# A third tile for block results, a later third sum, and two layer norms from statistics of halves, in a two-layer graph kernel

## The chip, the cores and the metric

The kernel runs on one core of one Trainium2 chip. A core has TensorE (PE: matrix products into PSUM; its weight loads are shown as PEld), VectorE (DVE), ScalarE (ACT), GpSimd (POOL, which here does nothing in layers 0 and 1 but issue gathers and scatters) and SyncE (SP, which issues the plain transfers). The metric is the device time of one execution in microseconds, the median of several runs; smaller is better.

## The reference

x has 2708 rows of 1024 float32, adj is a sparse 0/1 matrix of 2708 by 2708. Two layers follow each other, each with a residual and a layer norm:

```
# layer 0: attention over the neighbours in adj
q = x @ W_q.T + b_q;  k = x @ W_k.T + b_k;  v = x @ W_v.T + b_v
z = (q @ k.T) / sqrt(1024) * adj;   z = where(z == 0, -10000, z)
x1 = layernorm(x + relu(softmax(z) @ v))
# layer 1: sum over the neighbours
out = layernorm(x1 + adj @ (x1 @ weight) + bias)
```

The norm is (x - mean) / sqrt(var + 1e-5) over a row's 1024 elements, without weights.

## The kernel before

The work is cut into 22 blocks of 128 rows (the last, block 21, has 20). Because adj is sparse, each row's neighbours are listed, the rows are sorted by their number, and a block needs as many row gathers ("slots") as its fullest row has neighbours: `SLOTS` gives 15, 11, 8, ... for the blocks, 13 for block 8, 1 for blocks 18 to 20, 0 for block 21.

**Before 530 us** the kernel lists the neighbours, forms M = W_q.T W_k, and computes y = x M block by block (`y_block`), which is stored to DRAM in two parts, `y_ds`, for the first 8 blocks and the others. With y, a row's scores are dot products with the gathered rows of x.

**Layer 0, attention.** For a block, `attend` gathers y's rows (`gather_y`) and, slot by slot, rows of x (g tiles, 9 buffers, line 349), takes the scores on VectorE (line 792), turns them to probabilities, and sums the gathered rows with them into r (line 849). `flip` transposes r on TensorE (line 716), and r is multiplied by W_v. Blocks 0 to 6 and 21 do so alone (`project`, then `finish0`, lines 879 to 891); the other fourteen in seven pairs (`pairs`, first (7, 20), then (19, 18), last (13, 12)). For a pair the 2x2 block product over two blocks of rows and halves of the contraction and of the columns is done with seven half products instead of eight (`pair_products`, line 991 on; its matmuls are on line 976), which need four differences of the operands (`turn_pair`: S[0] to S[3] in s_all, lines 965 to 968) and four of the weights (lines 1107 to 1110). Each half product's PSUM bank is read out by an addition on VectorE at line 988 into a tile t. `finish_pair` adds the row of x with relu (line 1045), calls `norm` (lines 767 to 789) and scatters the block to x1 in DRAM (`scatter`, line 703). In `norm` ScalarE squares the whole row to get the variance (line 775), takes a logarithm and an exponential for the root (778, 780), VectorE mends these by one step (782 to 787), and ScalarE applies the norm to 1024 columns (788).

The tile t of the single blocks and of a pair's first block comes from the pool wp with two buffers; a pair's second comes from the pool xb with two. xb is opened where y's buffers (pool xa) lay, once y is done. A tile's next user waits until the scatter of the last one has landed.

**Layer 1, plain sums.** It works in units: (20,), (19, 18), (17, 16), (15, 1), ..., the last (12, 13). `sum_rows` gathers a block's neighbours of x1 and adds them up in r (lines 1209 and 1211), `gather_x1` fetches the block's own rows with the bias already in the tile (line 1218, then a gather that accumulates), `turn1` transposes and forms the differences, `work1` makes the products and adds the residual (line 1242), and `finish1` norms and scatters to the output. In the loop over units, unit i's products run after the next unit's transposes and after the sums for a unit further ahead have been put into the queues; the third unit's sums (got1[2]) are put ahead of the loop.

**What sets the order.** Each engine works through its queue in order. A scheduler lays the queues out from the program's order, from priorities (`tc.high_priority(URGENT)`, around evictions of PSUM) and from hints made with `follow`, which puts one instruction behind another on the same engine. So an instruction that waits holds up all that stand behind it on its engine.

Of the kernel before, what the change touches and what calls it, by code (L numbers as in the profile page):

```python
# [9 lines left out]
F32 = mybir.dt.float32  # L10
# [4 lines left out]
AF = mybir.ActivationFunctionType  # L15
ALU = mybir.AluOpType
# [4 lines left out]
P = 128  # L21
EPS = 1e-5
MASKED = -10000.0
FAR = 1.0e30
HALF = 512
# [55 lines left out]
def sparse_part(ctx, tc, x, xT, adj, wqT, wkT, wvT, bq, bk, bv, w1, b1, out):  # L81
    nc = tc.nc
    N, D = x.shape
    DC = D // P
    NH = D // HALF
    scale = 1.0 / math.sqrt(D)
# [11 lines left out]
    last = [b for b in range(NB) if SLOTS[b] == 0]  # L98
# [12 lines left out]
    with es:  # L111
        const = es.enter_context(tc.tile_pool(name="const", bufs=1))
        stat = es.enter_context(tc.tile_pool(name="stat", bufs=4))
# [34 lines left out]
        eps = const.tile([P, 1], F32, name="eps")  # L148
# [54 lines left out]
        loaded, sorted_, products, applied = [], [], [], []  # L203
# [54 lines left out]
        for c in range(DC):  # L258
            nc.vector.scalar_tensor_tensor(junk[:, :D], wq_i[c // 2][:, c % 2, :], scale, bk_bc, op0=ALU.mult,
                                           op1=ALU.mult, accum_out=u_col[:, c:c + 1])  # L260
# [75 lines left out]
        def follow(later, earlier, same=False):  # L336

            kind = mybir.DependencyClass.NoSync if same else mybir.DependencyClass.Sync
            tc.add_manual_dep(later.ins, earlier.ins.name, mybir.DependencyInfo(kind, mybir.DependencyReason.DATA),
                              reason="an engine's queue shall not stand still for a transfer")  # L340
# [346 lines left out]
        put = row_constants(0)  # L687
# [79 lines left out]
        def norm(t, sm, n, sm2=None):  # L767
# [20 lines left out]
            applied.append(nc.scalar.activation(t[:n], t[:n], AF.Identity, bias=nmr[:n], scale=rstd[:n]))  # L788
            return end

        def score(yg, xg, s, n):
            nc.vector.scalar_tensor_tensor(junkv[:n], yg[:n, :D], scale, xg[:n], op0=ALU.mult, op1=ALU.mult,  # L792
                                           accum_out=s)
# [84 lines left out]

        def finish0(b, po, xr):
            n = rows[b]  # L880
            t = wp.tile([P, D], F32, name="t")
            for h in range(NH):
                hs = slice(h * HALF, (h + 1) * HALF)
                with tc.high_priority(URGENT):
                    nc.vector.tensor_add(t[:n, hs], po[h][:n], bias_bc[:n, hs])
            sm = stat.tile([P, 1], F32, name="sm")
            nc.vector.scalar_tensor_tensor(t[:n], t[:n], 0.0, xr[:n], op0=ALU.max, op1=ALU.add, accum_out=sm[:n])
            end = norm(t, sm, n)
            scatter(x1_d[:, :], b, n, t, "x1")
            return end  # L890
# [60 lines left out]
            yield  # L951


        def turn_pair(flips, pool):

            A = []
            for k, flip_to in enumerate(flips):
                rT = (pool if k else wp).tile([P, DC, P], F32, name="rT", bufs=2)
                A.append(flip_to(rT))
            if len(flips) == 1:  # L960
                return A, None
            (a11, a12), (a21, a22) = [(a[:, :DC // 2], a[:, DC // 2:]) for a in A]
            s_all = wm_pool.tile([P, 4, DC // 2, P], F32, name="s_all", tag="m3")
            S = [s_all[:, i] for i in range(4)]
            nc.vector.tensor_add(S[0], a21, a22)
            nc.vector.tensor_sub(S[1], S[0], a11)
            nc.vector.tensor_sub(S[2], a11, a21)
            nc.vector.tensor_sub(S[3], a12, S[1])
            return A, S

        def differences():
# [8 lines left out]
        def halves_of(t):  # L980
            return t[:, :HALF], t[:, HALF:]
# [46 lines left out]
            return a[:, :DC // 2], a[:, DC // 2:]  # L1028

        def project_pair(pair, A, S):  # L1030
            ts = [(xb_pools[0] if k else wp).tile([P, D], F32, name="t", bufs=2) for k in range(2)]
            bias = halves_of(bias_bc)

            def whole(k, h, acc, what):
                add(halves_of(ts[k])[h], acc, what)

            pair_products(A, S, wv_q, wv_t, [bias, bias], [halves_of(t) for t in ts], whole, pair == pairs[-1])
            return ts

        def finish_pair(pair, ts):  # L1040
            for k, (b, t) in enumerate(zip(pair, ts)):
                xr, sums = pair_x[b], [stat.tile([P, 1], F32, name=f"sm{h}", bufs=6) for h in range(NH)]
                for h in (0, 1) if k == 0 else (1, 0):
                    th = halves_of(t)[h]
                    nc.vector.scalar_tensor_tensor(th, th, 0.0, halves_of(xr)[h], op0=ALU.max, op1=ALU.add, accum_out=sums[h])
                norm(t, sums[0], P, sums[1])
                scatter(x1_d[:, :], b, P, t, "x1")


# [144 lines left out]
        last_norm = applied[-1]  # L1194
        firsts = []

        def sum_rows(b, k=0):
            if b == "hub":
                n, tab, ok, r = P, tab_h, valid_h, part
            else:  # L1200
                n, tab, ok = (P, tab0, valid0) if b == 0 else (rows[b], tabs[:, b, :SLOTS[b]], valid[:, b, :SLOTS[b]])
                r = (cp if k else wp).tile([P, D], F32, name="r", bufs=RB)
            for j in range(tab.shape[1] if b else J0):
                if j == 0 and b not in [0, "hub"] + single + MIXED:
                    gather_slot(x1_d[:, :], tab[:n, 0:1], n, r)
                    continue
                xg = gather_slot(x1_d[:, :], tab[:n, j:j + 1], n, g_tile())
                if j == 0:
                    firsts.append(nc.vector.tensor_scalar(r[:n], xg[:n], ok[:n, 0:1], None, op0=ALU.mult))
                else:  # L1210
                    nc.vector.scalar_tensor_tensor(r[:n], xg[:n], ok[:n, j:j + 1], r[:n], op0=ALU.mult, op1=ALU.add)  # L1211
            return r

        def gather_x1(b, k=0):

            n = rows[b]
            xr = (cp if k else wp).tile([P, D], F32, name="xr", bufs=2 if k else 3)
            follow(nc.scalar.copy(xr[:n], bias1[:n]), last_norm, same=True)
            return gather_at(x1_d[:, :], tabs[:n, b, ROW:ROW + 1], n, xr, ALU.add)

        def finish1(b, t, sums):

            n = rows[b]
            if sums is None:
                sums = [stat.tile([P, 1], F32, name=f"sm{h}", bufs=6) for h in range(NH)]
                for h in range(NH):
                    nc.scalar.activation(junks[:n, :HALF], halves_of(t)[h][:n], AF.Copy, accum_out=sums[h][:n])
            norm(t, sums[0], n, sums[1])
            scatter(out, b, n, t, "out")

        def turn1(unit, rs):
# [3 lines left out]
        def work1(unit, A, S, xrs):  # L1235

            ts = [wp.tile([P, D], F32, name="t", tag="t" if k % 2 == 0 else "yg") for k, _ in enumerate(unit)]
            sums = [[stat.tile([P, 1], F32, name=f"sm{h}", bufs=6) for h in range(NH)] for _ in unit]

            def whole(k, h, acc, what):  # L1240
                with tc.high_priority(URGENT):
                    nc.vector.scalar_tensor_tensor(halves_of(ts[k])[h], acc, 1.0, what, op0=ALU.mult, op1=ALU.add,
                                                   accum_out=sums[k][h])

            xs_ = [halves_of(xr) for xr in xrs]
            if S is None:
                (a11, a12), x0 = halves_of_turned(A[0]), xs_[0]
                pa, pb = bank(), bank()
                half_products(pa, a11, w11, stop=False)
                add(x0[1], pa, x0[1])  # L1250
                half_products(pb, a11, t1, stop=False)
                half_products(pb, a12, w22, start=False)
                whole(0, 1, pb, x0[1])
                half_products(pa, a12, w21, start=False)
                whole(0, 0, pa, x0[0])
            else:
                pair_products(A, S, w1_q, w1_t, xs_, xs_, whole, unit == units[-1])
            return ts, sums
# [7 lines left out]
        nc.vector.tensor_sub(t3, t2, w11)  # L1266
        nc.vector.tensor_sub(t4, w21, t2)
        xrs = {0: [gather_x1(b, k) for k, b in enumerate(units[0])]}
        got1[2] = [sum_rows(b, k) for k, b in enumerate(units[2])]
        for i, unit in enumerate(units):  # L1270
            for p in pending:
                finish1(*p)
            if i + 1 < len(units):
                turned1[i + 1] = turn1(units[i + 1], got1.pop(i + 1))
                xrs[i + 1] = [gather_x1(b, k) for k, b in enumerate(units[i + 1])]
            if i + 3 < len(units):
                got1[i + 3] = [sum_rows(b, k) for k, b in enumerate(units[i + 3])]
            if i == 4:
                sum_rows("hub")
            pending = list(zip(unit, *work1(unit, *turned1.pop(i), xrs.pop(i))))  # L1280
            if i == 2:
                for b in last:
                    pending.append((b, gather_x1(b), None))
# [319 lines left out]
```

## Time and profile before

| | |
|---|---|
| time, median of 3 | 1079.57 us (1079.15 to 1083.0) |
| span of the profiled run | 1076.9 us |
| TensorE busy | 1007.8 us, 94% |
| VectorE busy | 847.2 us, 79% |
| ScalarE busy | 428.4 us, 40% |
| GpSimd busy | 490.7 us, 46% |
| layer 0's last product ends, layer 1's first transpose starts | 757.8, 770.3 us |
| last matmul ends, last scatter issued | 1058.8, 1064.0 us |

TensorE is busy for 94% of the span, so that the time is that of its products and of the few places in which it stands still. Such a place is found in the table of waits, and what ended it in the timeline: the number in brackets is the engine's idle time before the instruction, and after the arrow stands what released it. A share of busy time over the whole span tells little about a stage: VectorE is busy for 79% of it, but for nearly all of some stretches.

### The profile page before, as it was taken

How to read it: one execution, taken by the hardware profiler on the slowest of the kernel's cores; microseconds unless marked ns; L12 is line 12 of the kernel's file. 1: busy time of each engine (PE TensorE's matmuls, PEld its weight loads, DVE VectorE, ACT ScalarE, POOL GpSimd, SP SyncE). 2: the span in 40 equal slices, each digit the busy share in tenths (PEclk: the TensorE clock that was granted, in tenths of full speed). 3: DMA queues.
4: the chain of work that ended last, by engine and by line, in shares of the span. 5: the costliest groups of instructions: out<-in, count | busy, mean ns of one | idle time of the engine just before them, and what ended most of it. 6: DMA issues, size and time to landing. Idle time of an engine off the chain costs nothing.

```text
span 1076.9 us, 10217 instructions
## 1 busy us (share of the span) xinstructions
PE 1007.8 (94%) x2849; PEld 475.1 (44%) x2849; DVE 847.2 (79%) x1825; ACT 428.4 (40%) x898; POOL 490.7 (46%) x397
## 2 busy tenths in 40 slices
PE   7999999999998999999997999899489999999993
PEld 6444444444443444444543444444244444454441
DVE  8799999994388889998497999874578777887431
ACT  4688698422132332224433344332422363333322
POOL 1000140057564536435246566611477777887300
PEclk9999999999999999999998999999899999999997
DMA  9555457564886756796422677735589589969601
GB/s 355 199 206 203 173 196 273 170 244 125 300 279 225 240 191 189 229 334 198 149 92 86 205 255 268 235 118 193 167 284 256 199 269 324 293 204 329 179 39 42
DMA packets 90963, 229.20 MB, mean 213 GB/s; under 512 B 18410, under 2 KB 40394, under 8 KB 88188
## 3 DMA queue, kind: packets, MB, share of 16 engines
q0 software_dynamic: 48768, 148.05, 43.0%
q1 hardware_dynamic: 42128, 80.41, 21.7%
q8 instruction: 24, 0.39, 0.1%
q14 instruction: 43, 0.35, 0.1%
HBM read 219.61 MB, written 33.68 MB: 235 GB/s over the span
## 4 chain that ended last, share of the span: by engine, by line
PE 18%; issue 12%; DVE 11%; DMA 4%; POOL 3%; ACT 2%; POOLq 0%; DVEq 0%; ACTq 0%
PE po L976 16%; DVE junkv L792 2%; DVE r L849 2%; DMA g<-x_d,tabs 2%; DVE r L1211 1%; DMA yg<-y_d,tabs 1%; ACT junks L775 1%; DVE t L988 1%; POOL xr L343 1%; PE tr L716 1%; POOL g L349 1%; POOL x_d L703 1%; PE po L739 1%; PE tr L729 1%; POOL r L349 1%
## 5 line engine op out<-in xcount | busy, mean ns | idle before, releaser
L319 PE MATMUL po<-m_sb,xt 128*128 128x512 f32 x672 | 292.2, 594 | 3.3 <-DVE yo L323 3.3
L319 PEld LDWEIGHTS po<-m_sb,xt 128*128 128x128 f32 x672 | 126.4, 190 | 159.6 <-issue 150.8
L792 DVE SCALAR_TENSOR_TENSOR junkv<-yg,g 128x1024 uint8<-128x1024 f32 x109 | 133.1, 1221 | 36.3 <-DMA yg<-y_d,tabs 16.6
L349 POOL DMA_INDIRECT g<-in_x_dram,tabs x86 | 115.9, 1347 | 76.1 <-DVE r L849 19.4
L976 PE MATMUL po<-t,s_all 128*128 128x512 f32 x272 | 125.5, 604 | 10.9 <-DVE t L988 6.6
L1211 DVE SCALAR_TENSOR_TENSOR r<-g,valid,r 128x1024 f32<-128x1024 f32 x77 | 98.6, 1281 | 18.1 <-DMA g<-x_d,tabs 17.2
L609 PE MATMUL po<-wk_o,wq_o 128*128 128x512 f32 x256 | 110.5, 592 | 0.0
L775 ACT ACTIVATE junks<-t,lnm 128x1024 uint8<-128x1024 f32 (+1 forms) x43 | 49.3, 1146 | 135.2 <-DVE lnm L773 104.7
L739 PE MATMUL po<-wv,rT 128*128 128x512 f32 x224 | 97.7, 594 | 3.3 <-DVE pr L834 2.8
L976 PE MATMUL po<-w,rT 128*128 128x512 f32 x192 | 87.8, 607 | 0.0
L976 PEld LDWEIGHTS po<-t,s_all 128*128 128x128 f32 x272 | 52.0, 194 | 78.4 <-issue 60.7
L563 POOL DMA_INDIRECT tab_d<-rec,pos_i x22 | 27.1, 1230 | 129.9 <-DVE pos_i L552 123.5
L849 DVE SCALAR_TENSOR_TENSOR r<-g,pr,r 128x1024 f32<-128x1024 f32 x64 | 81.9, 1279 | 5.5 <-ACT r L861 4.6
L349 POOL DMA_INDIRECT g<-x_d,tabs x67 | 75.0, 1120 | 22.7 <-issue 15.5
L332 ACT ACTIVATE junka<-xt 128x128 f32<-128x128 f32 x176 | 53.8, 306 | 72.0 <-PE po L319 55.5
L788 ACT ACTIVATE t<-t,nmr,rstd 128x1024 f32<-128x1024 f32 (+1 forms) x43 | 52.6, 1238 | 73.8 <-DVE nmr L787 73.7
L224 DVE MAX8 few<-a 128x8 f32<-128x75 f32 (+3 forms) x132 | 79.2, 618 | 0.0
L609 PEld LDWEIGHTS po<-wk_o,wq_o 128*128 128x128 f32 x256 | 48.4, 190 | 59.3 <-issue 59.0
L976 PE MATMUL po<-w,s_all 128*128 128x512 f32 x160 | 72.1, 592 | 0.0
L221 DVE SCALAR_TENSOR_TENSOR a<-a,iota 128x2708 f32<-128x2708 f32 (+1 forms) x22 | 65.2, 2963 | 5.4 <-ACT junk L220 5.4
L739 PEld LDWEIGHTS po<-wv,rT 128*128 128x128 f32 x224 | 42.3, 190 | 56.3 <-issue 55.2
L219 ACT ACTIVATE junk<-a 128x2708 uint8<-128x2708 f32 (+1 forms) x22 | 54.1, 2459 | 24.7 <-DMA a<-in_adj_dram 20.1
(339 smaller groups left out, 1503.3 us busy)
## 6 DMA issues: line engine op xcount, KB each, us to landing
a<-in_adj_dram SPq DMA_DIRECT2D x21, 1354.0 KB, 5.9
xt<-in_xT_dram SPq DMA_DIRECT2D x21, 512.0 KB, 4.8
y_d<-yo SPq DMA_DIRECT2D x21, 512.0 KB, 5.7
g<-in_x_dram SPq DMA_DIRECT2D x21, 512.0 KB, 7.7
wq_i<-in_wqT_dram SPq DMA_DIRECT2D x8, 512.0 KB, 9.3
wk_i<-in_wkT_dram SPq DMA_DIRECT2D x8, 512.0 KB, 10.4
wv<-in_wvT_dram SPq DMA_DIRECT2D x16, 256.0 KB, 6.0
w<-in_w_dram SPq DMA_DIRECT2D x4, 1024.0 KB, 7.6
```

The lines of the kernel that those rows point to most:

```text
L219: nc.scalar.activation(junk[:n], a[:n], AF.Sign, accum_out=cnt[:n, b:b + 1])
L221: nc.vector.scalar_tensor_tensor(a[:n], a[:n], 1.0, iota[:n], op0=ALU.is_equal, op1=ALU.mult)
L224: nc.vector.max(few[:n, i * 8:(i + 1) * 8], a[:n, cuts[i]:cuts[i + 1]])
L319: put = nc.tensor.matmul(po, xt[:, c, :], m_sb[c // 2][:, c % 2, k0:k1], start=(c == 0), stop=(c == DC - 1))
L349: nc.gpsimd.indirect_dma_start(out=dst[:n], out_offset=None, in_=src, in_offset=bass.IndirectOffsetOnAxis(ap=at, axis=0), bounds_check=N - ...
L609: nc.tensor.matmul(po, wq_o[i // 2][:, o, i % 2 * P:(i % 2 + 1) * P], wk_o[:, o, hs], start=(o == 0), stop=(o == DC - 1))
L739: put = nc.tensor.matmul(acc, rT[:, c, :], w[c // 4][h][:, c % 4, :], start=(c == 0), stop=(c == DC - 1))
L775: nc.scalar.activation(junks[:n], t[:n], AF.Square, bias=nm[:n], accum_out=vs[:n])
L792: nc.vector.scalar_tensor_tensor(junkv[:n], yg[:n, :D], scale, xg[:n], op0=ALU.mult, op1=ALU.mult, accum_out=s)
L849: nc.vector.scalar_tensor_tensor(r[:n], xg[j][:n], pr[:n, j:j + 1], r[:n], op0=ALU.mult, op1=ALU.add)
L976: put = nc.tensor.matmul(acc, a[:, k], w[:, k], start=start and k == 0, stop=stop and k == DC // 2 - 1, skip_group_check=True)
L1211: nc.vector.scalar_tensor_tensor(r[:n], xg[:n], ok[:n, j:j + 1], r[:n], op0=ALU.mult, op1=ALU.add)
```

## The change

It has three parts.

- **A third tile.** The t of blocks 0 and 21 is now taken from xb, where t has three buffers instead of two. The wp pool's two buffers are then free for the first pairs, whose t need not wait for the scatters of blocks 0 and 21.
- **The third unit's sums.** got1[2] moves from ahead of the loop into its first turn, after the second unit's transposes, differences and own rows, and its first addition is put behind the last of the differences (S[3]) on VectorE.
- **The last norms.** For the second block of layer 0's last pair and of layer 1's last unit, the mean and variance come from VectorE's statistics of each half of the row, taken as each half is ready (`bn_stats`), and put together by `bn_aggr`. The norm's application is split: ScalarE does one half of the columns, VectorE the other. The computation of the root is the same.

```diff
+        def norm_halves(t, stats):
+            mv = stat.tile([P, 2], F32, name="mv")
+            nc.vector.bn_aggr(out=mv, in_=stats.rearrange("p h e -> p (h e)"))
+            lv = stat.tile([P, 1], F32, name="lv")
+            nc.scalar.activation(lv, mv[:, 1:2], AF.Ln, bias=eps)
+            near = stat.tile([P, 1], F32, name="near")
+            nc.scalar.activation(near, lv, AF.Exp, scale=-0.5)
...
+            applied.append(nc.scalar.activation(t[:, :HALF], t[:, :HALF], AF.Identity, bias=nmr, scale=rstd))
+            nc.vector.tensor_scalar(t[:, HALF:], t[:, HALF:], rstd, nmr, op0=ALU.mult, op1=ALU.add)
...
         def finish0(b, po, xr):
             n = rows[b]
-            t = wp.tile([P, D], F32, name="t")
+            t = xb_pools[0].tile([P, D], F32, name="t", bufs=3) if b in [0] + last else wp.tile([P, D], F32, name="t")
...
-            nc.vector.tensor_sub(S[3], a12, S[1])
+            halves_turned.append(nc.vector.tensor_sub(S[3], a12, S[1]))
...
-            ts = [(xb_pools[0] if k else wp).tile([P, D], F32, name="t", bufs=2) for k in range(2)]
+            ts = [(xb_pools[0] if k else wp).tile([P, D], F32, name="t", bufs=2 + k) for k in range(2)]
...
         def finish_pair(pair, ts):
             for k, (b, t) in enumerate(zip(pair, ts)):
+                ends = half_stats() if k and pair == pairs[-1] else None
...
+                    if ends is not None:
+                        nc.vector.bn_stats(out=ends[:, h, :], in_=th)
-                norm(t, sums[0], P, sums[1])
+                if ends is None:
+                    norm(t, sums[0], P, sums[1])
+                else:
+                    norm_halves(t, ends)
...
-        def sum_rows(b, k=0):
+        def sum_rows(b, k=0, behind=None):
...
+                if behind is not None:
+                    follow(put, behind, same=True)
+                    behind = None
...
+                    if k and unit == units[-1]:
+                        if len(sums[k]) == NH:
+                            sums[k].append(half_stats())
+                        nc.vector.bn_stats(out=sums[k][-1][:, h, :], in_=halves_of(ts[k])[h])
...
-        got1[2] = [sum_rows(b, k) for k, b in enumerate(units[2])]
         for i, unit in enumerate(units):
             for p in pending:
                 finish1(*p)
             if i + 1 < len(units):
                 turned1[i + 1] = turn1(units[i + 1], got1.pop(i + 1))
                 xrs[i + 1] = [gather_x1(b, k) for k, b in enumerate(units[i + 1])]
+            if i == 0:
+                got1[2] = [sum_rows(b, k, halves_turned[-1]) for k, b in enumerate(units[2])]
```

More of the change, by code (lines that the diff above doesn't have):

```diff
@@ L789, in norm, with half_stats @@
             return end
+        def norm_halves(t, stats):
[5 more added lines that the diff above has]
+            nc.scalar.activation(near, lv, AF.Exp, scale=-0.5)
+            ve = stat.tile([P, 1], F32, name="ve")
+            nc.vector.scalar_tensor_tensor(ve, mv[:, 1:2], EPS, near, op0=ALU.add, op1=ALU.mult)
+            nc.vector.tensor_scalar(ve, ve, near, -0.5, op0=ALU.mult, op1=ALU.mult)
+            rstd = stat.tile([P, 1], F32, name="rstd")
+            nc.vector.scalar_tensor_tensor(rstd, ve, 1.5, near, op0=ALU.add, op1=ALU.mult)
+            nmr = stat.tile([P, 1], F32, name="nmr")
+            nc.vector.scalar_tensor_tensor(nmr, mv[:, 0:1], -1.0, rstd, op0=ALU.mult, op1=ALU.mult)
+            applied.append(nc.scalar.activation(t[:, :HALF], t[:, :HALF], AF.Identity, bias=nmr, scale=rstd))
+            nc.vector.tensor_scalar(t[:, HALF:], t[:, HALF:], rstd, nmr, op0=ALU.mult, op1=ALU.add)
+        def half_stats():
+            return stat.tile([P, NH, nc.vector.BN_STATS_DIM], F32, name="halves", bufs=2)
         def score(yg, xg, s, n):
@@ L951, in attend_shares @@
             yield
+        halves_turned = []
         def turn_pair(flips, pool):
@@ L1208, in sum_rows @@
                 if j == 0:
-                    firsts.append(nc.vector.tensor_scalar(r[:n], xg[:n], ok[:n, 0:1], None, op0=ALU.mult))
-                else:
-                    nc.vector.scalar_tensor_tensor(r[:n], xg[:n], ok[:n, j:j + 1], r[:n], op0=ALU.mult, op1=ALU.add)
+                    put = nc.vector.tensor_scalar(r[:n], xg[:n], ok[:n, 0:1], None, op0=ALU.mult)
+                    firsts.append(put)
+                else:
+                    put = nc.vector.scalar_tensor_tensor(r[:n], xg[:n], ok[:n, j:j + 1], r[:n], op0=ALU.mult, op1=ALU.add)
+                if behind is not None:
+                    follow(put, behind, same=True)
+                    behind = None
             return r
@@ L1227, in finish1 @@
                     nc.scalar.activation(junks[:n, :HALF], halves_of(t)[h][:n], AF.Copy, accum_out=sums[h][:n])
-            norm(t, sums[0], n, sums[1])
+            if len(sums) == NH:
+                norm(t, sums[0], n, sums[1])
+            else:
+                norm_halves(t, sums[-1])
             scatter(out, b, n, t, "out")
```

## The prediction

> **What bounds the kernel now.** First the page's busy times, then TensorE's waits (columns: who waited, for whom, us in total, times, longest), since an edit off TensorE pays only where TensorE stood still.
>
> ```profile
> PE 1007.8 (94%) x2849; PEld 475.1 (44%) x2849; DVE 847.2 (79%) x1825; ACT 428.4 (40%) x898; POOL 490.7 (46%) x397
> ```
>
> ```profile
> PE tr L716 <- DVE r L1209: 13.7, 3, 12.5
> PE po L976 <- DVE t L988: 7.0, 2, 6.6
> PE po L976 <- DVE xr L988: 4.3, 3, 3.0
> ```
>
> TensorE is busy 94% of the span, and its three largest waits are where the change works: 12.5 us at the border of the layers, 6.6 us once in layer 0, 3.0 us once in layer 1. The timeline around the 6.6 us (start, length, engine, line, operation, and in brackets the idle time before it and its releaser):
>
> ```profile
> 569.87 7.48 POOL L349 DMA_INDIRECT g<-in_x_dram,tabs  x1 [0.30 <-DVE rstd L785]
> ...
> 578.89 1.00 POOL L703 DMA_INDIRECT x_d<-t,tabs  x1 [0.30 <-issue]
> ...
> 583.37 1.29 DVE L988 TENSOR_TENSOR t<-po,bias_bc 128x512 f32<-128x512 f32 x2 [6.90 <-DMA x_d<-t,tabs]
> 584.12 6.08 PE L976 MATMUL po<-t,s_all 128*128 128x512 f32 x8 [6.60 <-DVE t L988]
> ```
>
> VectorE reaches the first eviction of the first pair (block 7's t) and waits 6.9 us for the scatter of block 0, which still owns one of the two wp tiles named t. That scatter is issued only at 578.89, behind a gather that held GpSimd for 7.48 us. TensorE waits 6.6 us with it, and its next 8 matmuls take 6.08 us, where 8 take 3.60 elsewhere. The windows (length, busy time and count per engine, granted clock, DMA share, GB/s) tell who limits the stretch after it:
>
> ```profile
> 569.40:603.10 33.70, 27.10 (x64) 12.12 (x63) 25.40 (x52) 8.19 (x15) 19.77 (x12) 0.90 0.42 129
> 600.00:660.00 60.00, 59.68 (x170) 28.29 (x169) 59.61 (x133) 24.70 (x47) 39.33 (x31) 1.00 0.75 246
> ```
>
> From 600 to 660 us VectorE (third figure, 59.61 of 60) is as full as TensorE: what is won at 584 us is kept only as far as VectorE, too, runs earlier. TensorE's waits between 600 and 760 us confirm it: they are on VectorE's probabilities.
>
> ```profile
> PE tr L716 <- DVE pr L834: 2.4, 1, 2.4
> PE tr L716 <- DVE nms L819: 0.8, 1, 0.8
> ```
>
> Layer 1's start and the end:
>
> ```profile
> 786.32 1.29 DVE L1211 SCALAR_TENSOR_TENSOR r<-g,valid,r 128x1024 f32<-128x1024 f32 x1 [1.93 <-DMA g<-x_d,tabs]
> ...
> 789.80 1.99 PE L716 MATMUL tr<-ident,r 128*128 128x128 f32 x16
> ...
> 800.91 0.69 DVE L988 TENSOR_TENSOR xr<-po,xr 128x512 f32<-128x512 f32 x1
> ```
>
> ```profile
> 1058.84 0.69 DVE L1242 SCALAR_TENSOR_TENSOR t<-po,xr 128x512 f32<-128x512 f32 x1 [2.02 <-PE po L976]
> ...
> 1059.82 1.15 ACT L775 ACTIVATE junks<-t,lnm 128x1024 uint8<-128x1024 f32 x1 [2.95 <-DVE lnm L773]
> 1060.87 0.19 ACT L775 ACTIVATION_READ_ACCUMULATOR junks<-t,lnm 128x1 f32 x1
> 1061.09 0.29 ACT L778 ACTIVATE lv<-vs,eps 128x1 f32<-128x1 f32 x1
> ...
> 1062.49 1.24 ACT L788 ACTIVATE t<-t,nmr,rstd 128x1024 f32<-128x1024 f32 x1 [0.87 <-DVE nmr L787]
> 1064.00 0.95 POOL L703 DMA_INDIRECT out_dram<-t,tabs  x1 [5.91 <-ACT t L788]
> ```
>
> From the last eviction (1058.84) to the last scatter (1064.00) 5.16 us pass with nothing beside them; the same chain at the border runs from 757.75 to 763.64, 5.89 us.
>
> [...]6.08 against 3.60 us for 8 matmuls after the 6.6 us wait, 2.5 us of penalty. [...]the 7.48 us gather lay under L1109 and L1110 (two tensor_tensor of 2048, 2.3 us each) and ended 0.95 us after VectorE went idle, but at 609 to 615 us gathers took 1.0 to 1.4 beside two-input SCALAR_TENSOR_TENSORs. [...]
>
> **Part 1, the third tile t.** Blocks 0 and 21 take their t from the xb pool (now 3 buffers). So block 7 takes wp's t after block 2, block 19 after block 1, both scattered long before: the DMA wait is gone, and with it the 6.9 us. The xb tiles lie where layer 0's y buffers lay; in the built program block 21's first eviction now also waits for y's stores, but these had released a y gather at 526.87, and that eviction runs at 563: free. In the built order the pair's first L988 stands straight behind the second operands' last difference (569.4 us), and the pair's products run in their plain order.
> What follows, by durations of the trace: on VectorE from 569.4 to the second pair's first eviction lie 25.4 us of work in 33.7 us, so 8.3 us are idle (6.9 for the scatter, 1.1 for the cold matmuls, rest small). Going through the new order instruction by instruction I find VectorE at that eviction near 596 instead of 603.13, waiting for nothing: 7.1 to 7.5 us earlier. TensorE: the 4 products of 3.43 us from 572.2, with the fifth (a22 with t4) to 589.5, a transpose of 1.0 and two products of the next pair to 597.5, against 606.36: 8.9 us. The smaller counts, since VectorE is full until 660. Against it stands GpSimd: block 8's last gather, in the trace issued at 580.20, must land before VectorE wants it at 589. VectorE no longer goes idle at 576[...]. If a gather takes 2 us instead of 1, it is issued near 583 and lands near 588: just in time. Bounds: loss 0 to 4 us; I take 0.5. **Part 1: 6.8 us, from 3 to 8.9.** After 707 us TensorE runs without waiting to the layer's end, so that the gain is handed on whole.
>
> **Part 2, the third sums behind the second differences.** In the built order GpSimd now issues the second unit's two row gathers (xr, L1218's with accumulation) ahead of the third unit's four gathers, and VectorE makes the second differences before the third unit's two sums (L1211); the L988 that TensorE waits 3.0 us for keeps its place behind the fourth unit's sums, and these keep their place among the gathers. So 801.66 stays. What moves is the wait: the third unit's last gather goes from 779.24 to about 784.8, lands some 5 us after its issue ends, near 791, is summed by 792.4, and the transposes that began at 789.80 wait about 2.6 us; then 1 us of transposes and 7.03 us of products end near 800.8, where they meet the same L988. A wait of 3 us is turned into one of about 2.6 plus 0.9. **Part 2: 0, from a gain of 1 to a loss of 2.**
>
> **Part 3, norms by statistics of halves** (the pair's second block in both layers). Removed from the chain: lnm 0.25, Square 1.05 and its accumulator 0.22, so 1.52 us from 1059.57 to 1061.09. Added: one bn_stats of 512 behind the last eviction (no row of it; lower bound the 0.61 step of a 512 tensor_tensor, upper bound twice that, 1.2; I take 0.65, one pass over one input) and an aggregate, 0.25 like the small steps there: 0.9. The first half's statistics lie in a wait for TensorE (2.02 us before 1058.84), or, at the border, delay the other block's nmr by 0.6, whose scatter then issues near 758.9, before GpSimd is needed for the last. The apply goes from 1.24 on ScalarE to halves on two engines: about 0.65. Saving 0.6 + 0.55 = 1.15 each, 0.5 to 1.3. **Twice: 2.2 us**, both on the chain.
>
> **Sum.** 6.8 + 0 + 2.2 = 9.0 off 1079.57: about **1070.6 us**.
>
> **Rivals.** (a) A gather takes the scatter's place: VectorE at 589 us waits for block 8's last rows[...]; for it speaks the 7.48 us[...]. Part 1 then gives 3, the sum 5.2 or, with part 2 losing 1, 4: 1075.5. (b) VectorE is no limit after 600, since new slack appears at the two waits for yg (2.9 and 1.9 us): all 8.9 are kept, 8.9 + 2.2 + 0.5: 1068. (c) Slower: the denser stretch wins nothing (a new wait of 6.9 us elsewhere in the reordered 600 to 700), part 2 costs its 2 us and more because row gathers with accumulation stand before plain ones and DMA is 91% busy from 770 to 802, and statistics at 1.2 us save nothing: 1079.6 + 5 = 1085. Against it: no new wait of VectorE on a DMA that is late by the trace.
>
> **How the numbers follow.** Forecast 0.60, (a) 0.22, (b) 0.11, (c) 0.07. The bound of faster by over 0.5% is 1074.2: the forecast and (b) lie under it, with some of their spread over it, and a little of (a) under it: 0.74. Within 0.5%: 0.19; slower: 0.07. Range: from (b) less a little, 1066.5, to the middle of (a) and beyond, 1076.5.
>
> **What would show it.** Part 1 right: VectorE's wait for x_d<-t at L988 gone, no clock loss near 585, the second pair's first matmul on t2 near 597 to 598, and layer 0's last matmul near 751. Wrong: a wait of DVE for g or xr between 575 and 605, or TensorE waiting for transposes of block 8's r. Part 2: the 3.0 us wait on L988 becomes one on L716 for the third unit's r. Part 3: last eviction to last scatter 4.0 instead of 5.16. The prediction fails if bn_stats is far over 1.2 us, or if the reordered evictions cost TensorE new waits between 600 and 700.

## The result, and the profile after

The changed kernel takes 1067.62 us (median, 1065.79 to 1069.95) against 1079.86 us of the kernel before: a ratio of 0.9882, 95% interval 0.9855 to 0.991; the medians lie 12.2 us apart. The profiled span goes from 1076.9 to 1065.8 us. Line numbers shift: the products are L999 (L976 before), the evictions L1011 (L988), layer 1's sums L1238 and L1241 (L1209 and L1211), the score products L813 (L792), the row sums of attention L870 (L849). In what follows S0 to S3 are the differences of the operands, t1 to t4 those of the weights; xr are gathered rows of the residual, yg gathered rows of y.

Busy times and TensorE's waits of the changed kernel (who waited, for whom, us in total, times, longest):

```profile
PE 1007.5 (95%) x2849; PEld 475.1 (45%) x2849; DVE 850.6 (80%) x1831; ACT 425.4 (40%) x894; POOL 493.0 (46%) x397
```

```profile
PE tr L716 <- DVE r L1238: 12.0, 2, 11.7
...
PE tr L716 <- DVE r L870: 2.9, 4, 1.3
PE po L999 <- DVE xr L1011: 2.7, 1, 2.7
...
PE tr L716 <- DVE r L1241: 1.5, 1, 1.5
```

The wait for the evicted t (7.0 us before) is no longer in the table. The wait for layer 1's second xr is (2.7 after 3.0), and one for r at L1241 has joined it. The timeline of the changed kernel around the first pair:

```profile
570.48 0.68 DVE L1011 TENSOR_TENSOR t<-po,bias_bc 128x512 f32<-128x512 f32 x1
...
572.63 5.68 POOL L343 DMA_INDIRECT xr<-in_x_dram,tabs  x1 [0.67 <-DVE nmr L787]
573.30 3.60 PE L999 MATMUL po<-t,s_all 128*128 128x512 f32 x8
...
578.62 1.62 POOL L703 DMA_INDIRECT x_d<-t,tabs  x1 [0.30 <-issue]
...
595.32 0.68 DVE L1011 TENSOR_TENSOR t<-po,bias_bc 128x512 f32<-128x512 f32 x1
```

The first eviction carries no bracket: it waits for nothing. The scatter of block 0 is issued nearly as late as before (at 578.62 us for 578.89, though this kernel came to the pairs 1.1 us later), again behind a long gather (5.68 us); but nobody waits for it. The 8 matmuls on t2 take 3.60 us, not 6.08. The windows (length, then busy time and count of TensorE, its weight loads, VectorE, ScalarE, GpSimd, then the clock, DMA share and GB/s):

```profile
569.40:603.10 33.70, 33.70 (x86) 15.43 (x85) 33.70 (x70) 12.18 (x24) 24.68 (x15) 1.00 0.56 173
600.00:660.00 60.00, 59.51 (x168) 27.87 (x167) 59.58 (x136) 25.26 (x44) 41.69 (x33) 1.00 0.77 256
```

In the first stretch both engines are now busy without a gap (27.10 and 25.40 before) at full clock. To see what layer 0 gained as a whole, count from the last eviction of 20 rows before the pairs (564.93 before, 566.03 after) to layer 0's last eviction (757.75 and 748.94). First the kernel before, then the changed one:

```profile
564.93:757.75 192.82, 181.66 (x481) 83.65 (x479) 157.08 (x363) 68.22 (x128) 94.62 (x68) 0.98 0.58 194
```

```profile
566.03:748.94 182.91, 179.19 (x481) 82.59 (x479) 157.24 (x364) 68.05 (x128) 94.86 (x68) 1.00 0.62 205
```

The same 481 matmuls: the stretch is 9.91 us shorter, of which 2.47 are busy time (181.66 to 179.19: the mean clock is 1.00 for 0.98) and 7.44 idle time (11.16 to 3.72). VectorE's work is the same to 0.2 us. The end of the changed kernel:

```profile
1048.52 0.69 DVE L1278 SCALAR_TENSOR_TENSOR t<-po,xr 128x512 f32<-128x512 f32 x1 [1.43 <-PE po L999]
...
1049.26 0.69 DVE L1283 BATCH_NORM_STATS2 halves<-t 128x6 f32<-128x512 f32 x1
1049.98 0.21 DVE L794 BATCH_NORM_AGGREGATE mv<-halves 128x2 f32<-128x12 f32 x1
1050.23 0.29 ACT L796 ACTIVATE lv<-mv,eps 128x1 f32<-128x1 f32 x1 [3.68 <-DVE mv L794]
...
1051.62 0.81 ACT L806 ACTIVATE t<-t,nmr,rstd 128x512 f32<-128x512 f32 x1 [0.87 <-DVE nmr L805]
1051.62 0.55 DVE L807 TENSOR_SCALAR t<-t,rstd,nmr 128x512 f32<-128x512 f32 x1
1052.94 0.95 POOL L703 DMA_INDIRECT out_dram<-t,tabs  x1 [5.16 <-ACT t L806]
```

From the last eviction to the last scatter 4.42 us pass, 5.16 before. With such marks the spans can be cut into parts, here and for the experiments (us; each from the timelines, as told above; "border" is from layer 0's last eviction to layer 1's first transpose, "layer 1" from there to the last eviction):

| kernel | layer 0's pairs | border | layer 1 | end | time against before, 95% |
|---|---|---|---|---|---|
| before | 192.82 | 12.54 | 288.55 | 5.16 | |
| changed | 182.91 | 11.75 | 287.83 | 4.42 | 0.9882 (0.9855 to 0.991) |
| third tile alone | 182.54 | 12.52 | 291.25 | 5.17 | 0.9912 (0.9879 to 0.9946) |
| the same, two tiles | 185.28 | 12.54 | 288.41 | 5.17 | 0.994 (0.9922 to 0.9959) |
| norms alone | 192.79 | 11.78 | 289.59 | 4.41 | 0.9979 (0.9962 to 0.9995) |
| tile and norms | 182.73 | 11.76 | 289.49 | 4.42 | 0.9896 (0.985 to 0.9943) |
| later sums alone | 193.53 | 12.53 | 288.85 | 5.17 | 0.9999 (0.9976 to 1.0023) |
| changed, second profile | 182.96 | 11.76 | 290.88 | 4.42 | 0.9904 (0.9872 to 0.9936) |
| changed, third profile | 183.31 | 11.75 | 289.70 | 4.42 | 0.9866 (0.9834 to 0.9897) |
| sums later still | 182.76 | 11.77 | 295.19 | 4.41 | 0.99 (0.9865 to 0.9934) |
| S0 ahead of S1 | 182.57 | 11.76 | 291.72 | 4.42 | 0.9882 (0.9855 to 0.991) |

For the changed kernel's first profile: 9.91 + 0.79 + 0.72 + 0.74 = 12.2 us less, and 1.10 us more before the pairs, where nothing was changed; the two profiled spans are 11.2 us apart. On the three chips of the experiments the part before the pairs took 8 to 16 us longer than in the first profiles, for all kernels alike (the kernel before has medians of 1090 to 1094 us there); so the runs are compared by ratios to the kernel before on the same chip, and by the parts above.

### The profile page after: what moved, and what is told of

It is laid out like the page before. It is cut to its first block, busy times and chain, and to the rows that moved or that the text cites. A ratio compares the mean times of both kernels' runs of the same rounds, so it can differ in the third digit from the quotient of the medians.

```text
span 1065.8 us, 10216 instructions
## 1 busy us (share of the span) xinstructions
PE 1007.5 (95%) x2849; PEld 475.1 (45%) x2849; DVE 850.6 (80%) x1831; ACT 425.4 (40%) x894; POOL 493.0 (46%) x397
## 4 chain that ended last, share of the span: by engine, by line
PE 24%; DVE 12%; issue 5%; DMA 5%; POOL 3%; ACT 1%; POOLq 0%; DVEq 0%; ACTq 0%
PE po L999 21%; DVE r L870 3%; DMA g<-x_d,tabs 3%; DVE junkv L813 3%; DVE t L1011 1%; DMA yg<-y_d,tabs 1%; POOL g L349 1%; POOL xr L343 1%; PE tr L716 1%; PE po L739 1%; PE tr L729 1%; ACT junks L775 1%; DVE t L1069 1%; DVE r L1241 1%; DMA out_dram<-xr,tabs 0%
## 5 line engine op out<-in xcount | busy, mean ns | idle before, releaser
L813 DVE SCALAR_TENSOR_TENSOR junkv<-yg,g 128x1024 uint8<-128x1024 f32 x109 | 133.0, 1220 | 34.1 <-DMA g<-in_x_dram,tabs 16.7
L349 POOL DMA_INDIRECT g<-in_x_dram,tabs x86 | 110.7, 1288 | 72.3 <-DVE r L870 20.4
L999 PE MATMUL po<-t,s_all 128*128 128x512 f32 x272 | 124.3, 600 | 2.7 <-DVE xr L1011 2.7
L1241 DVE SCALAR_TENSOR_TENSOR r<-g,valid,r 128x1024 f32<-128x1024 f32 x77 | 98.6, 1281 | 19.1 <-DMA g<-x_d,tabs 18.3
L775 ACT ACTIVATE junks<-t,lnm 128x1024 uint8<-128x1024 f32 (+1 forms) x41 | 47.0, 1147 | 123.7 <-DVE lnm L773 95.2
L349 POOL DMA_INDIRECT g<-x_d,tabs x67 | 77.6, 1158 | 22.7 <-issue 12.8
L870 DVE SCALAR_TENSOR_TENSOR r<-g,pr,r 128x1024 f32<-128x1024 f32 x64 | 81.8, 1279 | 5.9 <-ACT r L882 4.6
L999 PE MATMUL po<-w,rT 128*128 128x512 f32 x192 | 86.4, 599 | 0.0
L999 PEld LDWEIGHTS po<-t,s_all 128*128 128x128 f32 x272 | 51.9, 192 | 68.5 <-issue 61.9
L788 ACT ACTIVATE t<-t,nmr,rstd 128x1024 f32<-128x1024 f32 (+1 forms) x41 | 50.0, 1237 | 81.2 <-DVE nmr L787 81.0
L999 PE MATMUL po<-w,s_all 128*128 128x512 f32 x160 | 72.1, 592 | 0.0
L717 ACT COPY rT<-tr 128x512 f32<-128x512 f32 x80 | 43.1, 586 | 56.1 <-PE tr L716 56.1
```

The source lines that it names most:

```text
L349: nc.gpsimd.indirect_dma_start(out=dst[:n], out_offset=None, in_=src, in_offset=bass.IndirectOffsetOnAxis(ap=at, axis=0), bounds_check=N - ...
L775: nc.scalar.activation(junks[:n], t[:n], AF.Square, bias=nm[:n], accum_out=vs[:n])
L870: nc.vector.scalar_tensor_tensor(r[:n], xg[j][:n], pr[:n, j:j + 1], r[:n], op0=ALU.mult, op1=ALU.add)
L999: put = nc.tensor.matmul(acc, a[:, k], w[:, k], start=start and k == 0, stop=stop and k == DC // 2 - 1, skip_group_check=True)
L1241: put = nc.vector.scalar_tensor_tensor(r[:n], xg[:n], ok[:n, j:j + 1], r[:n], op0=ALU.mult, op1=ALU.add)
```

## The experiments

**The third tile alone.** The kernel before with

```diff
-            t = wp.tile([P, D], F32, name="t")
+            t = xb_pools[0].tile([P, D], F32, name="t", bufs=3) if b in [0] + last else wp.tile([P, D], F32, name="t")
...
-            ts = [(xb_pools[0] if k else wp).tile([P, D], F32, name="t", bufs=2) for k in range(2)]
+            ts = [(xb_pools[0] if k else wp).tile([P, D], F32, name="t", bufs=2 + k) for k in range(2)]
```

> The kernel before with the third tile t alone (part 1); sums and norms as before. Theory (the wait for the scatter of block 0 held VectorE and TensorE, and most of what both win is kept): the wait of VectorE on x_d<-t at the first pair's first eviction is gone, the second pair's first product on t2 ends near 598 us instead of 606.4, layer 0's last eviction near 748 to 750 instead of 757.8, and the whole is 8 to 10 us under the kernel before. Rival 1 (VectorE, full after 600 us, gives a part of it back, as forecast): 6.8 us under. Rival 2 (the changed kernel's gain in layer 0 comes from the three parts together, by way of the order): under 4 us here.

Measured 1080.54 us against 1090.45, ratio 0.9912: 9.6 us less. Layer 0's pairs take 182.54 us, as in the changed kernel. The norms-alone kernel, profiled on the same chip with the tiles as before, takes 192.79 us there. So this part gives layer 0's whole gain. Rival 2 falls by the time (the interval is 5.9 to 13.2 us), rival 1, whose 6.8 us lie in that interval, by the trace alone: 10.3 us less in the pairs.

```profile
573.33:755.87 182.54, 179.33 (x481) 82.58 (x480) 156.67 (x363) 68.58 (x128) 95.30 (x68) 1.00 0.62 205
```

(Its absolute times in the trace are later than expected, since this chip came to the pairs 8.4 us later; from the pairs' start they fit.)

**The same with two tiles in the xb pool**, so that the wait comes back at another place (the edit is shown against the third tile alone):

```diff
-            t = xb_pools[0].tile([P, D], F32, name="t", bufs=3) if b in [0] + last else ...
+            t = xb_pools[0].tile([P, D], F32, name="t", bufs=2) if b in [0] + last else ...
...
-            ts = [(xb_pools[0] if k else wp).tile([P, D], F32, name="t", bufs=2 + k) for k in range(2)]
+            ts = [(xb_pools[0] if k else wp).tile([P, D], F32, name="t", bufs=2) for k in range(2)]
```

> As the third tile alone, in the same order of instructions on VectorE and TensorE, but the tiles named t of the xb pool are two instead of three, so that the second pair's first eviction on the third tile must wait for block 0's scatter. Theory (the wait counts, wherever it stands): a wait on x_d<-t of about 3 us comes back on VectorE near 580 us and 2 to 4 us of the 8 to 10 are lost. Rival (the new order of the evictions makes the gain, the wait is beside the point): no more than 0.7 us over the third tile alone.

Measured ratio 0.994, 6.5 us less: 3.1 us of the 9.6 are lost by the ratios, whose intervals overlap; by the trace layer 0's pairs take 2.74 us longer. The timeline of this kernel:

```profile
586.34 1.62 POOL L703 DMA_INDIRECT x_d<-t,tabs  x1 [0.30 <-issue]
...
590.84 0.69 DVE L988 TENSOR_TENSOR t<-po,bias_bc 128x512 f32<-128x512 f32 x1 [2.43 <-DMA x_d<-t,tabs]
591.59 3.70 PE L976 MATMUL po<-wv,s_all 128*128 128x512 f32 x8
```

VectorE's wait of 2.43 us for the same scatter costs 2.74 us, in the same order of instructions. The wait counts; the new order by itself does not make the gain. TensorE did not stand still in this wait: its next 8 matmuls follow within 0.1 us of the ones before and take 3.70 us. It loses the time later, where VectorE's lateness reaches it: its idle time in the pairs is 5.39 us, 3.21 with the third tile, and the mean clock of the stage is 1.00.

**TensorE kept busy in the wait.** The kernel before with 16 matmuls more, whose result is not used, ahead of the first pair's product on t2:

```diff
+            if warm:
+                mm = p_mm.tile([P, HALF], F32, name="mm")
+                for k in range(warm):
+                    put_ = nc.tensor.matmul(mm, ident, w21[:, k % (DC // 2)], start=True, stop=True)
...
+                put = half_products(pa, S[1], t2, start=False, stop=False, after=put_)
```

> The kernel before with 16 matmuls more on TensorE, whose result nothing reads, just ahead of the first pair's waiting product on t2; tiles as before, so that VectorE still waits for block 0's scatter. It asks what of the gain is the wait itself and what is TensorE's cold clock after it. Theory (VectorE's wait is the cause, the clock adds at most the 2.5 us that the cold matmuls show): the wait on x_d<-t stays near 6 us, TensorE's clock stays full, and the time falls by 0 to 2.5 us. Rival (TensorE's cold clock makes the loss, VectorE has time to spare): 5 us or more are won.

Both expectations were wrong: the ratio is 1.0087 (1.0055 to 1.0118), 9.5 us more. The timeline of this kernel:

```profile
581.73 7.03 PE L1007 MATMUL mm<-wv,ident 128*128 128x512 f32 x16
...
592.82 0.69 DVE L990 TENSOR_TENSOR t<-po,bias_bc 128x512 f32<-128x512 f32 x1 [6.82 <-DMA x_d<-t,tabs]
593.57 6.72 PE L976 MATMUL po<-t,s_all 128*128 128x512 f32 x8 [4.81 <-DVE t L990]
```

The added matmuls did not fill the wait. They took the place of S0 by t1 (3.60 us) and half a product of the next pair (1.88 us), which had filled TensorE's time ahead of it; these now came after it, a wait of 4.81 us stayed, and the 8 matmuls behind it were slow all the same (6.72 us; the mean clock from 594 to 630 us is 0.88). The stretch of the pairs grew from 192.82 to 202.75 us, TensorE's busy time in it by 10.2, its idle time not at all. Of the 10.2, 7.03 are the added matmuls; the other 3.1 are, by estimate, the clock's, whose mean over this stage is 0.97 in place of 0.98. So the clock's share was not measured by itself here. What this run does show is that the products in the order of the program (t2 ahead of S0 by t1), with the wait left in, win nothing.

**Norms alone** (the diff's `norm_halves`, `half_stats` and their calls, on the kernel before).

> The kernel before with the norms by statistics of halves alone (both last norms, part 3); tiles and sums as before. Forecast: 2.2 us under the kernel before (1.15 twice). Theory after the profile of the changed kernel (two chains 0.75 us shorter each, since ScalarE's half apply takes 0.81): 1.5 us under, layer 0 as before up to its last eviction near 757.8. Rival (the statistics cost as much as they save; what the changed kernel shows at these places is the start of the span): 0.3 us or less.

Measured ratio 0.9979 (0.9962 to 0.9995), 2.3 us, with 0.5 to 4 in the interval. The trace is sharper: border 11.78 for 12.54, end 4.41 for 5.16, together 1.5 us; the theory after the profile holds. The forecast's 2.2 us lie in the time's interval, but not in the trace.

**Tile and norms, without the later sums** (got1[2] back ahead of the loop).

> The changed kernel without part 2: third tile and norms by halves, the third unit's sums where they were. Theory A (part 2 is worth about 0.7 us): 10 to 10.5 us under the kernel before, against some 12 for the changed kernel with all three. Theory B (part 2 costs what layer 1's start lost, 1.5 us from its first transposes to the second unit's product on t2): 12.5 to 13.5 under. Forecast (0): as the sum of the other two runs of this call.

Measured ratio 0.9896, 11.3 us less; the changed kernel itself, with later sums, had 0.9882, 0.9904 and 0.9866 on three chips. No worth of part 2 can be told from these: the one lies amid the others.

**Later sums alone.**

```diff
-        got1[2] = [sum_rows(b, k) for k, b in enumerate(units[2])]
         for i, unit in enumerate(units):
...
+            if i == 0:
+                got1[2] = [sum_rows(b, k, halves_turned[-1]) for k, b in enumerate(units[2])]
```

> The kernel before with part 2 alone: the third unit's sums behind the second unit's last difference. Forecast: within 1 us of the kernel before, the 3.0 us wait of TensorE for the second unit's xr turned into one of about 2.6 us of the transposes for the third unit's r and 0.9 of work. Rival 1 (part 2 costs what layer 1's start lost in the changed kernel): the second unit's product on t2 starts 1.5 us later, and the whole is 1 to 2 us longer. Rival 2 (what is lost there is won back in the pairs after it): within 0.5 us, with the third to fifth units' products starting earlier by as much as the second unit's are late.

Measured ratio 0.9999 (0.9976 to 1.0023): no change, as forecast. Layer 1 took 288.85 us, 288.55 before; of the waits of the kernel from 765 to 900 us:

```profile
PE tr L716 <- ACT rT L717: 3.5, 2, 2.0
PE po L999 <- issue: 2.0, 1, 2.0
```

The 3.0 us wait before the second unit's product on t2 is 2.03 us here, and TensorE waits 1.46 us at the transposes ahead of it, where it did not before (the other 2.04 of the 3.5 us stand at 887 us, far behind). From layer 1's first transpose to that product lie 31.97 us, 31.37 before.

**The changed kernel again, on the chip of the kernel with the later sums alone.**

> The changed kernel once more, beside the other kernels of this call on one chip. Theory: the three parts add up (third tile 9.6 us, norms 1.5 to 2.3, part 2 about 0), so 11 to 12.5 us under the kernel before. If part 2 is worth 0.7 us or more by itself, 12.5 or over.

Measured ratio 0.9904, 10.5 us less: a little under the sum of its parts (9.6 + 2.3 + 0.1), within the interval. Its layer 1 takes 290.88 us where the first profile had 287.83, with the same program; half of these 3.05 us, 1.51, are TensorE's busy time, and the second unit's 8 matmuls on t2 took 6.70 us in place of 5.40 (last section). That is the spread against which the 0.72 us of the accounting has to be held.

**Sums later still.** A try for a better kernel: the fourth and fifth units' sums behind the second unit's products.

```diff
-            if i + 3 < len(units):
+            if 1 < i and i + 3 < len(units):
...
+            if i == 1:
+                for k_ in (3, 4):
+                    got1[k_] = [sum_rows(b, k) for k, b in enumerate(units[k_])]
```

> The changed kernel with the fourth and fifth units' sums of layer 1 written after the second unit's products instead of one unit earlier, so that the second unit's eviction into xr stands behind two units' sums fewer on VectorE, and the row gathers of these units come later on GpSimd. Theory (that eviction is late because sums whose rows are late stand before it): TensorE's 2.7 us wait for xr of the second unit falls under 1 us, and the time by 1 to 3 us against the changed kernel. Rival (layer 1's start is bound by the arrival of rows, whatever the order): the wait moves to the transposes of the fourth unit's r and the time is the same or longer.

The ratio is 0.99, no gain over the changed kernel beside it (0.9904), and layer 1 takes 295.19 us in the profile. VectorE's waits there:

```profile
DVE r L1241 <- DMA g<-x_d,tabs: 13.7, 5, 7.3
```

From layer 1's first transpose on VectorE stands 13.7 us for these gathered rows, once for 7.3; in the changed kernel beside it 6.2 us, at most 2.9 at once. With the gathers later, the rows are later, and the eviction behind them with them (TensorE's wait for xr is 5.3 us). The rival's first half holds, the rows bound this start; its place for the wait does not.

**S0 ahead of S1 in the second unit**, so that TensorE has other work while that eviction is late:

```diff
-                pair_products(A, S, w1_q, w1_t, xs_, xs_, whole, unit == units[-1])
+                pair_products(A, S, w1_q, w1_t, xs_, xs_, whole, unit in (units[1], units[-1]))
```

> The changed kernel with one more change: layer 1's second unit takes the order of products of the last unit, S0 by t1 ahead of S1 by t2, with a bank of its own for the last product, so that TensorE has 8 matmuls more to do while VectorE's first eviction of this unit stands behind the fourth unit's sums. Theory (in the changed kernel this eviction is late by 2.7 to 5.3 us, and the cold clock after it makes the next 8 matmuls 2 to 3 us longer): the wait for xr falls under 1 us, the matmuls after it take 3.6 us, and the whole is 3 to 6 us under the changed kernel of the same call. Rival (VectorE, which is late there, is late for the next products as well): the wait moves behind S0 by t1, to the eviction after it, and 0 to 1 us is won.

with the changed kernel beside it:

> The changed kernel unchanged, on the chip of the run before it, for the comparison. Theory: 10.5 to 12.5 us under the kernel before; the wait of TensorE for xr near the second unit's product on t2 between 2.7 and 5 us, as its gathers land.

Ratios 0.9882 and 0.9866: no gain. The timeline of the new kernel:

```profile
809.07 3.60 PE L999 MATMUL po<-t,s_all 128*128 128x512 f32 x8
...
815.75 0.68 DVE L1011 TENSOR_TENSOR xr<-po,xr 128x512 f32<-128x512 f32 x1
816.49 6.36 PE L999 MATMUL po<-w,s_all 128*128 128x512 f32 x8 [3.82 <-DVE xr L1011]
```

The product on t2 waits no more, but the eviction after it is late in its turn: 3.82 us, and the 8 matmuls behind it are slow (6.36 us). The rival holds: VectorE, which stood for rows for 16.1 us in this stretch (17.3 in the kernel beside it; 6.5 of each before layer 1's first transpose), is late for the next eviction too. No version was found that beats the changed kernel.

## Why the prediction came near, and where it was off

**The bound** was read rightly: the time is TensorE's, and its wait for the evicted t was worth taking away. The signs named for part 1 are all there: no wait of VectorE on x_d<-t, no loss of clock in the first pair (1.00), the second pair's first product on t2 at 598.2 ("near 597 to 598"), layer 0's last eviction at 748.9 (the last matmul was put "near 751").

**Part 1 was right in its mechanism and too small: 9.9 us, not 6.8.** Three terms of its sum:
- "7.1 to 7.5 us earlier" for VectorE at the second pair's first eviction. Counted from the pairs' start it comes at 29.29 us (566.03 to 595.32) and not at 38.20 (564.93 to 603.13): 8.91 us earlier. Between the first pair's first eviction at 570.48 and this one VectorE is busy for all of 24.84 us; "near 596" from 569.4 had meant 26.6. This is the term that was mis-sized. With 24.84 VectorE comes as early as TensorE alone could ("8.9 us"), so that the smaller of the two was no smaller.
- "I take 0.5" for gathers that land late, an estimate: none did. VectorE has no wait on a transfer between 566 and 605 us. The long gather did come back, as 5.68 us in place of 7.48, but ahead of the scatter, for which nobody waits now. It did not need VectorE to go idle: VectorE has no gap there now, and the gather ends at 578.31 us, 0.8 us after the second of the same two subtractions of 2048 columns. (Before, it ended 0.88 us after VectorE went idle, not 0.95.) What holds such a gather was not tested.
- The gain "handed on whole" from 707 us: yes, and 0.66 more between the second pair (9.25 us ahead on its first product on t2: 41.43 less 32.18 from the start of the pairs) and the end of layer 0 (9.91). TensorE's waits on probabilities of 2.4 and 0.8 us gave way to 2.9 in four small ones and 0.5, and VectorE's waits for yg shrank from 4.8 to 2.1 us. That slack is what rival (b) had pointed at; that its 1068 us came nearest is in part luck, as its 8.9 for part 1 was 1.0 too small and its 2.2 for part 3 0.7 too large.

The reasoning behind the first term was at fault more than the count: "what is won at 584 us is kept only as far as VectorE, too, runs earlier" is true, but VectorE, full from 600 to 660 both before (59.61 of 60) and after (59.58), did run earlier, because it had stood in the same wait. Here the full engine handed on its earlier start; it would have given back work that was added to it, and none was (157.08 and 157.24 us). By kind the 9.9 us are 6.6 + 0.4 of the wait itself, 2.5 of the clock after it (both as forecast, by the two windows above), and 0.4 of the smaller waits. In the kernel before TensorE did nothing from 577.52 to 584.12 us, and its clock was granted at half from 582.12 to 588.95; in the changed kernel the clock is 1.00 over the whole of the stage. In layer 1 waits of 2.67 and 3.04 us were followed by slow matmuls too (5.40 and 6.70 us for 8), one of 2.99 us was not (3.70; last section).

**Part 2, "0, from a gain of 1 to a loss of 2"**: nothing that can be measured, from the ratio 0.9999. The mechanism was half right. In the changed kernel the 3.0 us wait on L1011 became 1.54 us of transposes that wait for the third unit's r, and 2.67 us on the same L1011; "about 2.6 plus 0.9", with an eviction just met, was forecast. "So 801.66 stays" is 31.37 us after layer 1's first transpose; with the later sums it is 31.97 to 33.14 in four profiles, without them 31.37 to 34.04 in five. Both start in the same spread; that the rows' arrival makes it is likely from VectorE's waits for them, but was not tested. So layer 1's 0.72 us isn't shown to be part 2's.

**Part 3, "1.15 each": 0.77 at the border (from the last eviction to the scatter 5.89 us before, 5.12 after) and 0.74 at the end.** The first term was right: from the last eviction to the logarithm 2.25 us before (1058.84 to 1061.09) and 1.71 after (1048.52 to 1050.23), 0.54 less where 0.6 was forecast; a bn_stats of 512 takes 0.69 and the aggregate 0.21, for the assumed 0.65 and 0.25. The second was mis-sized: halving the apply was put at 0.55. From its start to the scatter are 1.51 us before (1062.49 to 1064.00) and 1.32 after, 0.19 less. ScalarE takes 0.81 us for 512 columns and 1.24 for 1024: half the work is two thirds of the time, and saves 0.43. The scatter then takes back half of that: it starts 0.50 us after ScalarE's apply ends, 0.28 before. In all profiles, at both places, it is 0.28 behind the apply on one engine and 0.48 to 0.50 behind that on two. The forecast had no term for this.

The sum of the forecast, 9.0, against 9.9 + 1.5 + 0 = 11.4 by the parts: one term 3.1 too small, another 0.7 too large. The other 0.7 or so of the parts' 12.2 us is layer 1's, and not assigned; the 1.10 us that the changed kernel lost before the pairs in its profile stand against it.

## What to carry to other kernels

Where two engines stand in the same wait, count the gain of both. Here all of it came back (9.9 us in layer 0's pairs, 2.5 of them of the clock after the wait): a partner that is full later is no brake, as long as its own start moves and no work is added to it. To halve an operation over two engines, first look up what the half takes (here 0.81 us of 1.24), and what its user then waits for. And before an effect of under 1 us is put down to an edit, look at how far the same program moves between two profiles: one stage here moved by 3 us.

## What the runs showed of the hardware beyond that

- Whether a wait was followed by a lower clock did not go by its length alone. Before the second unit's 8 matmuls on t2, in layer 1, waits of 2.54 us (changed kernel, third profile) and 2.99 us (kernel before) were followed by 3.70 us, but 2.67 (changed kernel) by 5.40 and 3.04 (its second profile) by 6.70. Below is first the stretch around the 2.99 us wait, in two halves, then, of the changed kernel, what lies ahead of the fall of the clock, 0.41 us behind the 2.67 us wait, and what lies behind it (length, then TensorE's busy time; the third figure from the end is the clock):

```profile
797.16:800.57 3.41, 1.50 (x4) 0.38 (x2) 3.33 (x5) 2.66 (x7) 2.58 (x3) 1.00 1.01 401
800.57:803.99 3.42, 2.33 (x6) 1.14 (x7) 3.42 (x5) 0.00 (x0) 2.73 (x3) 1.00 1.00 382
```

```profile
790.59:794.00 3.41, 0.74 (x2) 0.30 (x2) 3.37 (x6) 0.19 (x1) 2.91 (x2) 1.00 1.00 374
794.00:797.41 3.41, 3.41 (x5) 1.33 (x4) 3.41 (x7) 1.24 (x1) 2.50 (x2) 0.50 0.61 212
```

Ahead of the fall TensorE was busy for 0.74 of 3.41 us; around the 2.99 us wait, with no fall, for 3.84 of 6.83. A wait of 1.92 us (kernel before, from 876.65) was followed by half the clock, from 879.08 to 882.49. After the first 10 us and up to the last matmul, half the clock was granted for 6.83, 10.24 and 3.41 us in the kernel before, for 3.41, 13.65 and 3.41 in the changed one. What sets the moment of a change was not shown. With 5.40, 6.70 and 3.70 us in three profiles of one program, these 8 matmuls are a part of layer 1's spread.

- Statistics of 512 float32 columns took VectorE 0.69 us, as much as an eviction of that size (0.69), and putting two of them together 0.21.
- The two halves of the apply took 0.81 us on ScalarE and 0.55 on VectorE for 512 columns each, so that with this even split VectorE was done 0.26 us earlier.
